# Spectral layer: where and when its tables and tokens are loaded

## The chip, the cores and the metric

The kernel runs on one core of a Trainium2 chip. The metric is device microseconds of one launch. The time before is 2777.88 us, the median of three runs (2777.81, 2777.88 and 2810.39).

## The reference

Two layers act on `x` of shape (2, 128, 64, 64). Layer 0 is a group norm with four-head attention over 4096 tokens. Layer 1 turns each image into 4096 tokens of 128 channels, adds an attention of the normed tokens with themselves, and then adds a spectral layer:

```python
t = _to_tokens(x)
t = t + _L1_attn_ref(_ln_t(t))
t = t + _L1_ffn_ref(_ln_t(t), sigma, phi, M_u, M_phi_plus, M_phi_minus, log_weights, gumbel)
```

The spectral layer convolves the tokens causally with 16 filters of length 4096, once as they are and once with alternating signs, and mixes the 16 results by 128x128 matrices; a short three-tap part is added. Four branches (all, half, a quarter, an eighth of the tokens) are combined with weights of which one is nearly 1:

```python
U_plus = jnp.fft.irfft(Vf[None, :, :, None] * Uf_p[:, :, None, :], n=n, axis=1)[:, :sl]
out = jnp.einsum('btkd,k,kde->bte', U_plus, s, Mpp)
out = out + jnp.einsum('btkd,k,kde->bte', U_minus, s, Mpm)
```

## The kernel before

The program goes in order through layer 0 for both batches, the second attention of batch 0, that of batch 1 (`attend16`), and the spectral layer. A fast version of it, called with `in_halves` true, runs; a second version stands in the program for inputs whose ranges don't fit, and isn't executed here.

**Attention.** `attend16` goes over pairs (j, i) of blocks of 512 tokens, i from j on. For each pair TensorE computes scores from `bothT` (L1185: `hiT` and `loT`, two f16 parts of the normed tokens, transposed), ScalarE takes the exponential, and the result is weighed with `hi` and `lo`, the same tokens not transposed (L1213). For i > j the block is also needed transposed: SP issues two transposing DMAs `eT<-pair` (L1204), which are used two pairs later. Between these steps it calls `next(beside, None)`, which runs one piece of side work; beside batch 1's attention that is `feed(0, ...)`.

**feed(b)** prepares the spectral layer for batch b. For each of eight groups of four token tiles it normalises (`un`), transforms by two matmuls (L1328), splits the result into two f16 parts `uh` (two buffers), stores them in DRAM as `rows16[b]` by four DMAs each, makes `uT`, and computes the three taps into `oc` (one buffer, L1308 to L1315), which is stored as `base[b]` (L1316). Its DMAs are issued by GpSimd for batch 0 (`aside`) and by SP for batch 1. In pieces: one for `un`, two with `rows` stores, one for `uT`, three for the taps, seven in all for a group.

**The spectral layer** is 64 steps: 2 batches, 2 halves `ro` of the output rows, 8 chunks `ch`, 2 signs `s`. A step needs two halves of tables (a tile of [128, 16, 8, 32] f16 each, 1 MB, read from DRAM `tables16` by one DMA) and two halves of tokens ([128, 8, 128] f16, by two DMAs of 128 KB from `rows16[b]`). `convolve16` multiplies them (16 matmuls, L1541, in four turns w of four; turns 0 and 1 use the first half, 2 and 3 the second); ScalarE and VectorE turn the results into f16 parts `x`. `mix16` then runs 48 matmuls (L1557) with the matrices `mxr` and `mxl`. The mix of a step is laid between the four turns of the next step's convolution, and one piece of side work is taken from `beside` in each turn. TensorE's order is written out: `ordered` is `tc.keep_in_program_order`, which pins an instruction behind the instruction traced just before it on its engine. Instructions that aren't pinned are placed by a planner, which lets them float to where it takes their inputs to be ready.

Side work of the first 16 steps is `feed(1, ...)`, after four empty pieces. After each (batch, ro) follows `back`, which turns the 16 chunks back into tokens: five empty pieces, then for each of four parts a load `had<-base` (L1653, one buffer), four plus four transposes, and an inverse transform (L1669) that VectorE adds to `had` (L1671). After `ro` 1 the result goes out by four DMAs.

**Loads of a step.** `chunk16(n, ...)` is called at the start of step n. Tables and tokens have two sets, by n % 2. Set 0 of the tables, `tables_a`, lies in a pool `early`, opened after batch 0's attention; set 1, `tables_b`, takes the places b0 and b1 of the pool `px`, where `hi` and `lo` lay. Tables are issued by SP (L1483), tokens by GpSimd (L1478), those of step 0 by SP. None of these DMAs is pinned. Each waits until the convolution of step n − 2 has read its half.

SP and GpSimd issue in order: an issue that waits holds back what stands behind it on that engine. `px` also has a place a, which holds `bothT` during the attentions. `transform` loads `fw` (L975) on GpSimd, and `closed(j)`, called at the end of a row of the attention, lets VectorE and GpSimd (`lrsf`, a power, L108) finish the norm of batch 1's tokens.

Of the kernel before, what the change touches and what calls it, by code (L numbers as in the profile page):

```python
# [13 lines left out]
F16 = mybir.dt.float16  # L14
# [8 lines left out]
P = 128  # L23
B, C, HH, WW = 2, 128, 64, 64
# [11 lines left out]
NK = 16  # L36
# [3 lines left out]
BP = NI // 2  # L40
NF = P
NW = NF // 4
NDI = 2 * BP - 1
# [3 lines left out]
NCH = NW // WC  # L47
NS = NF // NCH // 2
# [28 lines left out]
def conv_attn_hybrid(ctx: ExitStack, tc: tile.TileContext, io):  # L77
    nc = tc.nc
# [31 lines left out]
    def pool(stack, name, bufs=1, **kw):  # L110
        return stack.enter_context(tc.tile_pool(name=name, bufs=bufs, reuse_waits="tile", **kw))
# [5 lines left out]
    def chain(*parts):  # L117
        for p in parts:
            yield from p
# [588 lines left out]
    tables16 = dram.tile([2, NF // NS, 2, 2, 2, NDI, NS, 2 * NK], F16, name="tables16")  # L708
    rows16 = [dram.tile([2, 2, DROWS, NF, C], F16, name=f"rows16_{b}") for b in range(B)]
# [48 lines left out]
    def layers(st, layer0, in_halves):  # L758
# [3 lines left out]
        tokens = [pool(st, f"tok{b}", side="right") for b in range(B)]  # L762
        tok = [tokens[b].tile([P, NI, C], F32, tag="t", name=f"tok{b}") for b in range(B)]
        px = pool(st, "px", side="right")
# [196 lines left out]
        psum, bank = banks(psum_a)  # L961
# [18 lines left out]
        if not in_halves:  # L980
            tokens_in = ffw.tile([P, 2, 2, WC // 2, C], F32, name="tokens_in")
# [77 lines left out]
        def attend(b, p, beside, closed, ready=lambda i: None):  # L1059
# [111 lines left out]
            for _ in beside:  # L1171
                pass

        def attend16(b, p, beside, closed):

            den = p.tile([P, NT, NQ], F32, tag="den", name=f"den{b}")
# [205 lines left out]
        with ExitStack() as l1:  # L1382
            p1 = pool(l1, "l1")
            if not in_halves:
                lo.append(p1.tile([P, L], F32R, name="lo"))
            with ExitStack() as part:
                p = pool(part, "l1_a")
                gate = [0]

                def second_parts(n):  # L1390
                    if n < NQ and not in_halves:
                        low = p.tile([P, 2, 512], F32, tag="low", name=f"low{n}")
                        nc.sync.dma_start(low, lows[n].rearrange("n p c -> p n c"))
                        copy = nc.vector.tensor_copy(loT[0][:, bass.ts(n, 512)], low[:, 0])
                        if n == 0:
                            tc.keep_in_program_order(copy)
                        nc.vector.tensor_copy(lo[0][:, bass.ts(n, 512)], low[:, 1])

                def ready(i):
                    second_parts(i + 1)  # L1400

                second_parts(0)
                fw = transform(p1)

                def closed(j):
                    gate[0] = j + 1

                y = [None]

                def stage(i, n):  # L1410
                    y[0] = p.tile([P, 512], F32, tag="y", name=f"y1_{i}")
                    return y[0]

                stats = LayerStats(p1, tok[1], "a1")
                own = (rest16(p),) if in_halves else (filters(p, fw), matrices(p))
                steps = chain(left, stats.steps(), *own, normalise(1, stats, stage, gate))
                (attend16(0, p1, steps, closed) if in_halves else attend(0, p1, steps, closed, ready))
            right0.close()
            if in_halves:
                early = pool(middle, "early", side="right")  # L1420
                tables_early = [early.tile([P, BP, NS, 2 * NK], F16, name=f"tables_a{n}") for n in range(2)]
                tokens_in = [
                    [early.tile([P, NS, C], F16, name=f"tokens{turn}_{n}") for n in range(2)] for turn in range(2)
                ]
            if in_halves:
                mxr, mxl = mixing
            else:
                mxr, mxl = (x[0].rearrange("p (k s c) -> p k s c", k=NK, s=2) for x in (hiT, loT))
            with ExitStack() as part:
                p = pool(part, "l1_b", 2)  # L1430
                fed = LayerStats(ffw, tok[1], "f1")

                def closed(j):
                    fed.take(range(4 * j, 4 * j + 4))
                    fed.close(range(4 * j, 4 * j + 4))
                    own = slice(2 * j, 2 * j + 2)
                    m = p.tile([P, 2, 2, C], F32, tag="m", name=f"m{j}")
                    aside.dma_start(m, mx[own].rearrange("k p s c -> p k s c"))
                    nc.vector.tensor_copy(mxr[:, own], m)
                    nc.vector.tensor_tensor(mxl[:, own], m, mxr[:, own], ALU.subtract)  # L1440

                (attend16 if in_halves else attend)(1, p1, feed(0, p, bank, fw), closed)
        psum_a.close()


# [2 lines left out]
        late_pool = pool(right1, "late", 2, side="right")  # L1448

        if in_halves:  # L1450
            tables_in = [
                tables_early,
                [px.tile([P, BP, NS, 2 * NK], F16, tag=f"b{n}", name=f"tables_b{n}") for n in range(2)],
            ]
        else:
            tables_in = [
                px.tile([P, 2, WC // 2, 2 * BP * NK], F32, tag=f"b{n}", name=f"tables_in{n}") for n in range(2)
            ]

        def ordered(instruction):  # L1460
            return tc.keep_in_program_order(instruction)

        def one_bank(name):
            return pc.tile([P, 512], F32, tag="bk", name=name)

        STREAM = {(0, 0): 0, (0, 1): 2, (1, 0): 1, (1, 1): 0}
        FIRST = (0, BP + 1, BP)

        def chunk16(n, b, ro, ch, s):

            row = FIRST[STREAM[ro, s]]
            halves = []
            for half in range(2):
                w0 = 2 * NS * ch + NS * half
                tt = tables_in[n % 2][half]
                ut = tokens_in[n % 2][half]
                for copy in range(2):
                    (nc.gpsimd if n else nc.sync).dma_start(  # L1478
                        ut[64 * copy : 64 * copy + 64],
                        rows16[b].rearrange("h c r w d -> (h c) r w d")[:, row : row + BP, w0 : w0 + NS, :],  # L1480
                    )
                own = tables16[s, w0 // NS]
                nc.sync.dma_start(  # L1483
                    tt,
                    bass.AP(
                        tensor=own.tensor,
                        offset=own.offset,
                        ap=[[NDI * NS * 2 * NK, 8], [NS * 2 * NK, BP], [1, BP * NS * 2 * NK]],
                    ),
                )  # L1490
                halves.append((tt, ut))
            return halves

        def chunk(turn, b, ro, ch, s):


            row = FIRST[STREAM[ro, s]]
            halves = []
# [194 lines left out]
        fw = transform(late_pool)  # L1693
        beside = chain([None] * WC, feed(1, late_pool, one_bank, fw, fed))
        steps = 0
        for b in range(B):
            for ro in range(2):
                oh = (late_pool if ro else tokens[0]).tile(
                    [P, L], F32, tag="oh" if ro else "t", name=f"oh{b}_{ro}", bufs=1
                )  # L1700
                for ch in range(NCH):
                    acc = pc.tile([P, 512], F32, tag="acc", name=f"m{b}_{ro}_{ch}")
                    for s in range(2):
                        u = f"{b}_{ro}_{ch}_{s}"
                        if in_halves:
                            xs = [
                                pf.tile([P, NK, 512], F16, tag=f"x{n}", name=f"x{n}_{u}", bufs=2) for n in range(2)
                            ]
                            parts = convolve16(u, chunk16(steps, b, ro, ch, s), *xs)
                        else:  # L1710
                            halves = chunk(steps % 2, b, ro, ch, s)
                            xh = pf.tile([P, NK, WC * 4 * 2 * BP], F32R, tag="xh", name=f"xh{u}", bufs=2)
                            parts = convolve(steps, u, halves, xh)
                        for _ in parts:
                            next(late, None)
                            next(beside, None)
                        late = mix16(ch, s, *xs, acc, oh) if in_halves else mix(steps, ch, s, xh, acc, oh)
                        steps += 1
                for _ in beside:
                    pass  # L1720
                if (b, ro) == (0, 0):
                    right1.close()
                    late_pool = pool(right1, "out", 2, side="right")
                beside = back(b, ro, oh, outs, late_pool)
                if in_halves and (b, ro) == (0, 1):
                    beside = chain(beside, guard(one_bank))
# [136 lines left out]
```

## Time and profile before

The profile is of one execution that took 2786.72 us; its span, from the first to the last instruction, is 2784.9 us, at a mean granted TensorE clock of 0.977.

| what | before |
|---|---|
| median of three runs | 2777.88 us |
| profiled execution | 2786.72 us, span 2784.9 |
| first convolution of step 0 starts | 1724.7 us |
| first convolution of step 1 starts | 1746.3 us |
| `m` L1557, 3072 matmuls | 622.5 + 391.4 us busy |
| `x` L1549 on VectorE, 512 | 602.3 us busy, 1219 ns each |
| `tables_a`, `tables_b`, 64 + 64 transfers of 1 MB | issued by SP |
| `tokens`, 252 transfers of 128 KB | issued by GpSimd, 12.2 us to landing |
| `rows<-uh` of batch 1, 64 of 64 KB; `base<-oc`, 8 of 256 KB; `had<-base`, 12 of 256 KB | issued by SP |
| DMA queue of SP | 231.71 MB of 311.92 MB |

How to read such a profile: the times are microseconds from the span's start. "PE" is TensorE's matmuls, "PEld" its weight loads, "DVE" VectorE, "ACT" ScalarE, "POOL" GpSimd, "SP" SyncE; "SPq" is SP's sequencer, which issues DMAs. A name such as `tables_b<-tables` is the written tile and the read one. The chain of waits is followed back from the last instruction: at each step to what released it. A wait is put down to the releaser that came last. The windows give busy time of each engine in a stretch, the granted clock as a share of full speed, and the mean busy share of the 16 DMA engines.

### The profile page before, as it was taken

What the parts mean: (1) busy time and instruction counts of PE and PEld (TensorE: products, weight loads), DVE (VectorE), ACT (ScalarE), POOL (GpSimd) and SP (SyncE); (2) the same over time, 40 slices, a digit from 0 to 9 for tenths busy, and PEclk for the clock granted to TensorE, in tenths of its full rate; (3) what the DMA queues carried; (4) which work ended last, traced back from release to release, by engine and by line L of the source; (5) the groups of instructions that cost most, each with busy time, mean ns of one, the idle gap of its engine ahead of it and who ended that gap; (6) DMA issues with size and microseconds to landing.
All of it is one profiled execution on the core that took longest, in us unless ns stands there. A gap on an engine that the chain in (4) does not pass through costs nothing.

```text
span 2784.9 us, 32561 instructions
## 1 busy us (share of the span) xinstructions
PE 2588.1 (93%) x11955; PEld 1276.1 (46%) x11955; DVE 1668.5 (60%) x2946; ACT 1841.3 (66%) x2059; POOL 432.5 (16%) x711
## 2 busy tenths in 40 slices
PE   5999999999998996999989988898789999999998
PEld 3555555555544452444434443343344445445444
DVE  5256564246267225767886567575456666666664
ACT  4999999999998894556644555454345555555553
POOL 2022121012124201100043100111111111111110
PEclk9999999999999997999999998999999999999999
DMA  4122220012014307655375654666666666655662
GB/s 144 35 65 67 65 65 20 7 50 74 22 39 94 67 5 135 115 107 105 69 144 110 126 96 91 154 174 156 149 167 165 200 192 181 179 206 179 185 188 87
DMA packets 351051, 311.92 MB, mean 112 GB/s; under 512 B 292816, under 2 KB 303200, under 8 KB 334432
## 3 DMA queue, kind: packets, MB, share of 16 engines
q1 hardware_dynamic: 295376, 231.71, 32.6%
q0 software_dynamic: 52512, 74.81, 11.2%
q10 hardware_dynamic: 2992, 3.22, 0.4%
q8 instruction: 96, 1.57, 0.2%
q14 instruction: 75, 0.61, 0.1%
HBM read 212.53 MB, written 23.33 MB: 85 GB/s over the span
## 4 chain that ended last, share of the span: by engine, by line
PE 30%; DMA 13%; DVE 7%; issue 1%; ACT 1%; POOL 0%; SPq 0%; DVEq 0%; ACTq 0%; POOLq 0%
PE m L1557 19%; PE cv L1541 6%; DMA eT<-pair 5%; DMA tables_b<-tables 3%; DVE pair L1199 3%; DMA base<-oc 2%; DVE both L1232 2%; PE ar L1312 1%; DMA had<-base 1%; DVE x L1549 1%; PE bk L1669 1%; DMA tables_a<-tables 1%; DMA rows<-uh 1%; PE od L1213 1%; PE pf L1328 0%
## 5 line engine op out<-in xcount | busy, mean ns | idle before, releaser
L465 ACT ACTIVATE e<-s 128x1536 f16<-128x1536 f32 (+1 forms) x704 | 938.4, 1427 | 52.9 <-PE s L209 48.3
L1549 DVE TENSOR_TENSOR x<-cv,x 128x1024 f16<-128x1024 f32 x512 | 602.3, 1219 | 302.9 <-ACT x L1548 302.9
L1548 ACT CAST x<-cv 128x1024 f16<-128x1024 f32 x512 | 493.7, 1017 | 404.4 <-PE cv L1541 389.5
L1557 PE MATMUL m<-x,mxr 128*128 128x512 f16 x2048 | 622.5, 381 | 0.0
L209 PE MATMUL acc<-e,v 128*97 128x512 f16 x2048 | 559.0, 380 | 16.4 <-DVE accs L413 13.7
L209 PE MATMUL s<-qs,ks 128*128 128x512 f16 x2048 | 559.7, 380 | 7.9 <-ACT e L465 4.3
L1557 PE MATMUL m<-x,mxl 128*128 128x512 f16 x1024 | 391.4, 382 | 3.3 <-DVE oh L1564 3.2
L209 PEld LDWEIGHTS <-v 128*97 128x97 bf16 x2048 | 255.4, 125 | 229.8 <-issue 28.9
L1194 ACT ACTIVATE ey<-y,nshift 128x512 f32<-128x512 f32 x288 | 196.0, 685 | 225.3 <-PE y L1185 135.9
L1557 PEld LDWEIGHTS <-mxr 128*128 128x128 f16 x2048 | 201.3, 98 | 242.8 <-issue 5.3
L209 PEld LDWEIGHTS <-ks 128*128 128x128 f16 x2048 | 201.0, 99 | 229.6 <-issue 46.8
L1478 POOL DMA_DIRECT2D tokens<-rows x252 | 152.9, 611 | 845.5 <-PE cv L1541 819.8
L1232 DVE SCALAR_TENSOR_TENSOR both<-eT 128x512 f16<-128x512 f16 x224 | 153.6, 686 | 135.2 <-DMA eT<-pair 124.5
L1213 PE MATMUL od<-pair,hi 128*128 128x512 f16 x576 | 189.6, 391 | 30.0 <-DVE oT L1225 15.1
L1185 PE MATMUL y<-bothT 128*128 128x512 f16 x864 | 206.5, 381 | 4.0 <-ACT ey L1194 3.0
L1199 DVE TENSOR_TENSOR pair<-ey,pair 128x1024 f16<-128x1024 f32 x144 | 175.4, 1218 | 16.0 <-ACT pair L1198 15.6
L413 DVE COPY accs<-acc 97x512 f32<-97x512 f32 x64 | 44.1, 689 | 227.3 <-PE acc L209 227.1
L1541 PEld LDWEIGHTS <-tokens 128*128 128x128 f16 x1024 | 100.6, 99 | 164.5 <-issue 68.1
L1213 PEld LDWEIGHTS <-hi 128*128 128x128 f16 x1024 | 102.6, 100 | 146.2 <-issue 35.1
L1198 ACT CAST pair<-ey 128x1024 f16<-128x1024 f32 x144 | 150.2, 1043 | 24.6 <-DMA eT<-pair 11.4
L1557 PEld LDWEIGHTS <-mxl 128*128 128x128 f16 x1024 | 101.0, 99 | 131.6 <-DVE oh L1564 10.0
L1213 PE MATMUL oa<-eT,hi 128*128 128x512 f16 x448 | 146.6, 389 | 14.3 <-DMA eT<-pair 14.3
(221 smaller groups left out, 2297.5 us busy)
## 6 DMA issues: line engine op xcount, KB each, us to landing
tables_a<-tables SPq DMA_DIRECT2D x64, 1024.0 KB
tables_b<-tables SPq DMA_DIRECT2D x64, 1024.0 KB
tokens<-rows POOLq DMA_DIRECT2D x252, 128.0 KB, 12.2
tab<-in_rot SPq DMA_DIRECT2D x32, 512.0 KB
ks<-term POOLq DMA_DIRECT2D x112, 64.0 KB, 2.2
qs<-term POOLq DMA_DIRECT2D x112, 64.0 KB, 2.1
accs<-back SPq DMA_DIRECT2D x32, 128.0 KB
room<-in_mpp POOLq DMA_DIRECT2D x16, 256.0 KB, 3.4
```

The source lines that it names most:

```text
L209: tc.keep_in_program_order(nc.tensor.matmul(*args, **kw))
L465: nc.scalar.activation(e[:, own, :], ps[:, own, :], AF.Exp, scale=SCORE_SCALE)
L1185: nc.tensor.matmul(ps[:, q, :], a[0][:, bass.ts(t, P)], c[0][:, bass.ts(i, 512)], start=(n == 0), stop=(n == 2),)
L1194: nc.scalar.activation(e[:, q, :], ps[:, q, :], AF.Exp, bias=nshift16, accum_out=den[:, t, i : i + 1])
L1199: nc.vector.tensor_tensor(pair[:, 1, own], e, pair[:, 0, own], ALU.subtract)
L1213: nc.tensor.matmul(acc, a[0][:, own], pair(m, t), start=(start and t == 0 and n == 0), stop=(stop and t == 3 and n == 2),)
L1232: nc.vector.scalar_tensor_tensor(both, eT[:, 0, :, u, :], 1.0, eT[:, 1, :, u, :], ALU.mult, ALU.add, accum_out=den[:, 4 * i + u, j : j + 1],)
L1478: (nc.gpsimd if n else nc.sync).dma_start(ut[64 * copy : 64 * copy + 64], rows16[b].rearrange("h c r w d -> (h c) r w d")[:, row : row + B ...
L1541: ordered(nc.tensor.matmul(pu[:, h, :], ut[:, at, :], tt[:, :, at, :], start=True, stop=True))
L1548: nc.scalar.copy(hi, pur)
L1549: nc.vector.tensor_tensor(lo, pur, hi, ALU.subtract)
L1557: nc.tensor.matmul(acc, m, x, start=(s == 0 and i == 0), stop=(s == 1 and i == len(products) - 1))
```

## The change

`chunk16` goes. A generator `fetch16(n, queue)` and a small `halves16(n)` take its place, defined before the attention:

- Tables and tokens have three sets, by n % 3. Set 0 of the tables is in `early` as before (now `tables_e`), set 1 is one tile `second` in `px`'s place a, set 2 takes places b0 and b1. The third set of tokens is in `early`.
- Step n now begins with `fetch16(n + 1, nc.sync)`, so the loads of step n + 1 stand ahead of step n's convolution and side work. For n = 63 it returns at once.
- All loads are pinned by `ordered`. Tokens are always issued by GpSimd, tables by the queue that is given.
- `fetch16(0, nc.gpsimd)`, tables and tokens of step 0, is appended to the side work of batch 1's attention, behind `feed(0, ...)`; one piece for each half.

```diff
+        def fetch16(n, queue):
+            if n == len(STEPS):
+                return
+            b, ro, ch, s = STEPS[n]
+            row = FIRST[STREAM[ro, s]]
+            for half in range(2):
+                w0 = 2 * NS * ch + NS * half
+                tt, ut = halves16(n)[half]
+                for copy in range(2):
+                    ordered(
+                        nc.gpsimd.dma_start(
+                            ut[64 * copy : 64 * copy + 64],
+                            rows16[b].rearrange("h c r w d -> (h c) r w d")[:, row : row + BP, w0 : w0 + NS, :],
+                        )
+                    )
+                own = tables16[s, w0 // NS]
+                ordered(
+                    queue.dma_start(
+                        tt,
...
+                    )
+                )
+                yield
+
+        def halves16(n):
+            return list(zip(tables_in[n % 3], tokens_in[n % 3]))
...
-                (attend16 if in_halves else attend)(1, p1, feed(0, p, bank, fw), closed)
+                if in_halves:
+                    attend16(1, p1, chain(feed(0, p, bank, fw), fetch16(0, nc.gpsimd)), closed)
+                else:
+                    attend(1, p1, feed(0, p, bank, fw), closed)
...
-            tables_in = [
-                tables_early,
-                [px.tile([P, BP, NS, 2 * NK], F16, tag=f"b{n}", name=f"tables_b{n}") for n in range(2)],
-            ]
+            second = px.tile([P, 2, BP, NS, 2 * NK], F16, tag="a", name="tables_a")
+            tables_in.append([second[:, n] for n in range(2)])
+            tables_in.append([px.tile([P, BP, NS, 2 * NK], F16, tag=f"b{n}", name=f"tables_b{n}") for n in range(2)])
...
-        def chunk16(n, b, ro, ch, s):
...
-                for copy in range(2):
-                    (nc.gpsimd if n else nc.sync).dma_start(
...
-                            parts = convolve16(u, chunk16(steps, b, ro, ch, s), *xs)
+                            for _ in fetch16(steps + 1, nc.sync):
+                                pass
+                            parts = convolve16(u, halves16(steps), *xs)
```

## The prediction

> **What bounds the kernel now.** I read the page first: what is busy, and at which clock.
>
> ```profile
> span 2784.9 us, 32561 instructions
> PE 2588.1 (93%) x11955; PEld 1276.1 (46%) x11955; DVE 1668.5 (60%) x2946; ACT 1841.3 (66%) x2059; POOL 432.5 (16%) x711
> PE   5999999999998996999989988898789999999998
> PEclk9999999999999997999999998999999999999999
> ```
>
> TensorE is busy 93%; the weak slices inside are the 16th (1044 to 1114 us) and most from the 24th to the 30th (1601 to 2089). In the 16th layer 0 ends and batch 0's second attention starts; the spectral layer runs from 1724.6 to the end. The windows say how much TensorE time lies idle where (columns: stretch, length, busy of each engine, granted clock, DMA share, GB/s).
>
> ```profile
> 1098.40:1109.00 10.60, 1.03 (x3) 0.25 (x2) 0.00 (x0) 0.88 (x4) 0.00 (x0) 0.66 0.74 147
> 1724.60:1746.20 21.60, 7.20 (x19) 1.97 (x17) 13.06 (x31) 7.90 (x8) 4.55 (x6) 0.62 0.59 131
> 1752.00:2124.80 372.80, 336.33 (x1508) 159.12 (x1506) 226.29 (x241) 169.14 (x192) 48.45 (x80) 0.97 0.62 160
> 2124.80:2291.70 166.90, 166.28 (x769) 74.86 (x768) 114.82 (x100) 93.93 (x99) 29.08 (x48) 1.00 0.61 192
> 2371.90:2420.10 48.20, 43.83 (x194) 18.94 (x193) 28.91 (x26) 23.12 (x24) 7.27 (x12) 0.96 0.60 173
> 2420.10:2743.40 323.30, 322.27 (x1537) 152.12 (x1536) 222.30 (x195) 178.32 (x190) 50.91 (x84) 1.00 0.58 182
> ```
>
> Fourth and sixth row: where steps have little side work, idle is under 0.4%, and nothing can be won. What can be won is idle 9.6 us (first row), 14.4 (second), 36.5 (third), 4.4 (fifth), 65 in all, and some slow clock. TensorE's waits from 1720 on and the chain name the releasers.
>
> ```profile
> PE cv L1541 <- DMA tables_b<-tables: 24.8, 8, 12.3
> PE ar L1312 <- ACT oc L1308: 11.5, 3, 8.2
> PE cv L1541 <- DMA tables_a<-tables: 7.5, 3, 2.9
> ...
> 1723.93 22.22 DMA tables_b<-tables
> ...
> 1889.39 23.22 DMA base<-oc
> ...
> 2029.06 29.16 DMA tables_b<-tables
> ```
>
> Tables cost 32.3 us directly. `oc` waits for its own store, which took 23.2 us for 256 KB because SP's queue also held tables. Last, SP's issues in order of time, early and at the border:
>
> ```profile
> 1084.26 1.48 SPq L1483 DMA_DIRECT2D tables_a<-tables  x2
> 1087.73 51.21 SPq L1204 DMA_TRANSPOSE eT<-pair  x9
> ...
> 1708.12 4.74 SPq L1204 DMA_TRANSPOSE eT<-pair  x2
> 1723.28 1.24 SPq L1483 DMA_DIRECT2D tables_b<-tables  x2
> 1729.87 4.68 SPq L1483 DMA_DIRECT2D tables_a<-tables  x2
> ```
>
> Step 0's tables are issued at 1084, 640 us before use and just ahead of transposes that batch 0's attention needs at once; step 1's only at 1723.3.
>
> The packet records of the trace add a rate: a half of a step's tables is 128 packets of 8,192 bytes, and the halves pass SP's queue one after another. From the first packet of step 1 (1724.7) to the last of step 21's first-issued half pair (2121.0) 42 halves pass; the queue is empty between halves for 13.4 us in all. So a half takes (396.3 − 13.4) / 42 = 9.1 us, two 18.2, while a step with side work takes TensorE 16.4 to 17.3 where it doesn't stall. In that stretch the tables' stream itself is about as long as TensorE's work. Later, alone, a half takes 5.5 to 8.5 us and a bare step 13.8.
>
> **The change part by part.** The sum is made against the profiled execution: 2786.72 us (span 2784.9), 8.8 above the median 2777.88; I take the difference over to the median unchanged.
>
> *Step 0's tables leave 1084.* Gone: 9.6 us idle at 1098.4 to 1109, 1.1 in the 7 us behind it, and about 3 of half clock (6.9 us busy at 0.54 to 0.66). Without the 2 MB, the stretch 1160 to 1200 still idles 2.3 in 40, 0.6 per 10. Gain 11; bounds 5 (the stall is partly the transposes' own) and 13.
>
> *They come back on GpSimd beside batch 1's attention,* at about 1572 to 1580, when the first feed ends: four token issues (0.61 us each, as in L1478's row) and two of tables on POOL, which is busy 1.3 us of the 10 from 1570 on. Behind them in POOL's order wait the next `lrsf` power (next due 1617) and `fw`, with 40 us to spare. SP loses four token issues (2.24 us at 1547). The 2 MB are wanted at 1724: landing costs nothing. What they do to the transposes isn't in the trace. From below: 0, being in another queue than the transposes. From above: 14, all that the same bytes cost at 1084. I take 4, nearer the lower end, since at 1084 the halves took 20.9 us and the transposes stood behind all of it in one queue. The Trainium skill's "DMA: Bandwidth & Descriptors" (Queues, rings and completion order) speaks against this part: all queues share the same engines, which take turns between queues by packets. By that rule the transposes would go at half rate for some 20 us, an estimate of 10 instead of 4, and the sum would be 6 smaller.
>
> *Step 1 moves to the buffer of `bothT`* (tag a), whose last reader is the last L1185 at 1710.3 to 1713.0; before, it waited for `hi` and `lo`, read until 1723.4. SP has nothing between its last transposes (1708.1) and this. So the issue moves from 1723.3 to 1713. Step 1's tokens hang behind `fw`'s load on POOL (1577 before), so they remain early. Step 1 began at 1746.3, right behind its second half (last packet 1744.6); I expect 1736, when x of step 0 is done (DVE until 1736.6). Counted in the next part.
>
> *Three sets, issued ahead of side work.* What it doesn't remove is bytes. A fetch of step n+1 is pinned behind the SP transfers traced in step n−1 and no longer waits for step n−1's matmuls, only for step n−2's. The stream begins at 1714.4 instead of 1724.7 and loses its empty stretches. With 42 halves at 9.1 it would end at 2097, at 9.9 at 2130. 9.9 is the mean of the 14 halves issued within 0.9 us of each other (8.1 to 12.3), and pairs are what the new order issues beside side work. I take 9.4: 1714.4 + 395 = 2109; step 21 needs the first of its halves, 9.4 earlier, plus 1.6 to signal it: 2101 against 2124.8. Gain 23 for this part and step 1 together. Bounds: 3 (at 9.9: 2122) and 66 (no stall: 14.4 + 36.5 idle, 15 slow clock at 0.62, 0.65 and 0.97). The page's section Bandwidth gives 6.15 us for 1 MB; by that 42 halves would take 258 us, an estimate, and the sum would be that of the first rival. The rows here (0.52 to 0.62 of the engines' time, 125 to 160 GB/s) decide against it.
>
> *Side transfers then queue behind tables.* What is behind a fetch on SP: the `rows`, `base` and `had` transfers of its own step; what is ahead: those of the step before. A `base` store stands behind one fetch's rest, as now, so its present cost (11.5 us) stays inside the sum; more of it is the slow rival.
>
> *Step 38 to 40:* idle 4.4, where `out` stores fill the queue; one more step of lead (some 14 us, against waits of 2 to 3) covers it. Gain 4 (0 to 5). Bare steps: the halves are still freed 6.9 us apart; no change. Register and instruction counts of TensorE, DVE and ScalarE stay.
>
> Sum: 11 + 23 + 4 − 4 = 34; 2786.7 − 34 = 2753 for a profiled execution, 2744 for the median.
>
> **The rivals.** *TensorE alone bounds the layer.* The third set lets halves overlap side work so freely that they run at the later rate (5.5 to 8.5 us each). For it: halves 12 to 15 took 5.9 to 8.7 in the middle of side work. Against: most there took 8.1 or more. Then 56 of the 66 go (10 stay for `oc` and `uh`): 11 + 56 + 4 − 3 = 68, median 2710.
>
> *The stream stays the bound.* Pairs at 9.9: gain 3; GpSimd's 2 MB cost 10: 11 + 3 + 4 − 10 = 8, median 2770. This is also the case that the change doesn't do what it says: the tables are asked for sooner, and arrive no sooner.
>
> *Slower: stores and loads of side work stuck behind two whole fetches.* `oc` has one buffer; from its store to the next write are five of the seven turns of a row group, 5 × 4.3 = 21.5 us. The three stores in the chain took 22.3 to 23.2 and cost 11.5; from 21.5 on, every microsecond of queue is TensorE's. `had` has one buffer too: twice it took 14.3 to 16.6, and VectorE waited up to 6.1. If all 7 later stores cost 8.2 and the 9 later loads of the three turns 6.1, that is 57 + 55 − 24 (paid now: 11.5 and 12.8) = 88 more. Against 11, 4 and 10 (step 1), and 4 lost: 67 slower, median 2845.
>
> **How the numbers follow.** Chances: forecast 0.46 (its own range 2725 to 2765), TensorE alone 0.22 (2700 to 2725), stream 0.18, slower 0.14 (2785 to 2860). The range 2704 to 2785 holds the forecast, the stream rival and nearly all of the fast rival, and leaves out the slow one. 2% is 55.6 us, about what a measurement of this kernel can tell from no change: faster than 2722 is the fast rival but its edge, and the forecast's tail, 0.24; slower than 2833 is somewhat over half of the slow rival, 0.08; the rest 0.68.
>
> **What would show it.** Step 0's tables on POOL near 1575, and no idle of 9 us near 1100: part one. A wait for `eT` over 5 us soon after 1575: its cost. Step 1 beginning 10 us after step 0's last convolution or less: the border. From there to step 21, the interval, 378.5 now from step 1, near 365 with the queue never empty: the stream; near 325: the fast rival; waits on `oc` or `had` above 30 us in sum: the slow one. I am wrong if the halves' mean leaves 8.5 to 9.9 us, or if the scheduler moves attention's own work when it places the new transfers.

## The result, and the profile after

The changed kernel takes 2805.89 us (median of 20 executions, 2782.06 to 2828.83); the kernel before, beside it, 2788.08 (20 executions, 2771.6 to 2814.15). The ratio is 1.0059, with a 95% interval of 1.0033 to 1.0084: slower by under 1%, where 2744 us was predicted and 2785 was the upper end of the range. Ratios here leave out, on both sides, executions more than 1.5% above the fastest of their kernel, so they are not exactly the quotient of the medians.

The profiled execution of the changed kernel took 2782.06 us, the lowest of its 20, so its total flatters it. A second profile of the same code, called "again" below, took 2804.88 (span 2803.1) and is near the median. The page of the first:

```profile
span 2780.2 us, 32560 instructions
...
PE 2586.0 (93%) x11955; PEld 1275.8 (46%) x11955; DVE 1669.1 (60%) x2946; ACT 1841.9 (66%) x2059; POOL 437.3 (16%) x717
...
PE   5999999999999997989989689899999999999998
...
PEclk9999999999999998999999899999999999999999
```

In the row of TensorE (PE) the weak slice where layer 0 ends is better (the 16th, 7 instead of 6), and a new hole stands in the 23rd slice (the 6, at 1529 to 1599 us), inside batch 1's attention. The windows of the changed kernel, cut where the work changes, tell more. The columns are the stretch, its length, busy time of TensorE, of weight loads, of VectorE, ScalarE and GpSimd, then clock, DMA share and GB/s.

```profile
1043.20:1354.20 311.00, 276.87 (x1269) 126.13 (x1268) 234.09 (x537) 174.27 (x360) 17.57 (x20) 0.96 0.56 107
1556.70:1739.70 183.00, 145.61 (x649) 64.40 (x648) 107.65 (x249) 87.41 (x180) 13.97 (x21) 0.93 0.70 110
1739.70:1749.50 9.80, 6.54 (x19) 1.86 (x18) 9.74 (x25) 7.08 (x8) 3.31 (x4) 0.72 0.52 116
1749.50:2110.40 360.90, 337.47 (x1525) 160.94 (x1525) 232.73 (x249) 172.10 (x195) 49.84 (x82) 0.98 0.62 166
```

And the same windows of "again", where step 1 to step 21 is the last row:

```profile
1047.70:1357.90 310.20, 277.94 (x1268) 126.18 (x1268) 233.77 (x537) 174.36 (x360) 17.55 (x20) 0.96 0.57 107
1559.90:1742.50 182.60, 147.29 (x649) 64.86 (x648) 107.67 (x249) 87.23 (x180) 13.94 (x21) 0.92 0.70 110
...
1752.30:2138.00 385.70, 346.98 (x1525) 163.04 (x1525) 232.13 (x249) 171.58 (x195) 49.43 (x82) 0.95 0.62 156
```

Beside the kernel before, in us:

| stretch | before | changed | again |
|---|---|---|---|
| batch 0's second attention | 323.1 | 311.0 | 310.2 |
| 217th score block of batch 1 to step 0 | 155.2 | 183.0 | 182.6 |
| step 0 to step 1 | 21.6 | 9.8 | 9.8 |
| step 1 to step 21 | 378.5 | 360.9 | 385.7 |
| step 21 to step 40 | 280.9 | 290.7 | 283.6 |
| step 40 to step 63 | 330.4 | 331.0 | 333.3 |

So the gain of 12 in batch 0 and of 12 at the border is there. Batch 1's attention gives 27 to 28 back, and from step 1 on nothing is won for certain: the two profiles of one program differ by 25 us in steps 1 to 21. In "again", the one near the median, the rows add up to a loss of 15.5 us.

The waits of TensorE in the changed kernel, from 1740 us on:

```profile
PE cv L1554 <- DMA tokens<-rows: 12.0, 6, 4.4
PE cv L1554 <- DMA tables_e<-tables: 8.0, 5, 3.2
PE cv L1554 <- DMA tables_a<-tables: 6.8, 3, 3.1
PE cv L1554 <- DMA tables_b<-tables: 5.5, 3, 2.7
```

Together 32.3 us; before, tables alone were 24.8 + 7.5 = 32.3. The wait for `oc`, 11.5 before, is gone. And in batch 1's attention TensorE waits for transposes. From 1280 to 1740 us in the changed kernel:

```profile
PE oa L1254 <- DMA eT<-pair: 23.4, 4, 17.0
```

and from 1280 to 1724 us in the kernel before:

```profile
PE oa L1213 <- DMA eT<-pair: 0.9, 1, 0.9
```

The cause stands in the order of time. GpSimd's issues in the changed kernel (start, duration):

```profile
1558.13 1.31 POOL L1194 DMA_DIRECT2D tokens<-rows  x2
1559.43 0.60 POOL L1201 DMA_DIRECT2D tables_e<-tables  x1
1561.10 1.23 POOL L1194 DMA_DIRECT2D tokens<-rows  x2 [1.07 <-issue]
1562.32 0.60 POOL L1201 DMA_DIRECT2D tables_e<-tables  x1
...
1577.56 1.82 POOL L1194 DMA_DIRECT2D tokens<-rows  x3 [7.38 <-DMA tables_e<-tables]
```

and the chain that ended last, in the same kernel, with the transposes that it passes through:

```profile
1547.53 5.03 DMA eT<-pair
...
1558.38 12.28 DMA eT<-pair
...
1584.26 19.54 DMA eT<-pair
...
1642.70 4.31 DMA eT<-pair
```

A transpose that takes 4.3 us later in the same attention takes 12.3 and 19.5 while GpSimd's tables and tokens pass; the next block pairs wait. Besides the 2 MB of tables and step 0's tokens, GpSimd issues eight loads there, the tokens of steps 1 and 2 (the x3 in the row at 1577.56 are some of them). Those of step 1 were loaded in the kernel before too, at 1563.5, ahead of this stretch, which begins at 1569.5 there; those of step 2 come this early because there is a third set.

### The profile page after: what moved, and what is told of

Same layout as the page of the kernel before. It is cut to its first block, busy times and chain, and to the rows that moved or that the text cites. A ratio compares the mean times of both kernels' runs of the same rounds, so it can differ in the third digit from the quotient of the medians.

```text
span 2780.2 us, 32560 instructions
## 1 busy us (share of the span) xinstructions
PE 2586.0 (93%) x11955; PEld 1275.8 (46%) x11955; DVE 1669.1 (60%) x2946; ACT 1841.9 (66%) x2059; POOL 437.3 (16%) x717
## 4 chain that ended last, share of the span: by engine, by line
PE 55%; DMA 20%; DVE 14%; ACT 7%; issue 3%; SPq 0%; POOL 0%; DVEq 0%; ACTq 0%; POOLq 0%
PE m L1570 18%; PE acc L209 11%; PE s L209 11%; DMA eT<-pair 9%; PE cv L1554 6%; ACT e L465 5%; DVE pair L1240 4%; DMA tables_e<-tables 3%; DVE both L1273 3%; DMA tables_b<-tables 2%; PE od L1254 1%; DMA tables_a<-tables 1%; PE y L1226 1%; PE ar L1353 1%; DMA tokens<-rows 1%
## 5 line engine op out<-in xcount | busy, mean ns | idle before, releaser
L1240 DVE TENSOR_TENSOR pair<-ey,pair 128x1024 f16<-128x1024 f32 x144 | 175.5, 1219 | 16.6 <-ACT pair L1239 16.3
```

The costliest lines, as they stand in the source:

```text
L1240: nc.vector.tensor_tensor(pair[:, 1, own], e, pair[:, 0, own], ALU.subtract)
```

## The experiments

The interval in each is of its ratio to the kernel before, run beside it. A stretch is read from one profile of each, and "again" shows how far two profiles of one program lie apart: 0.4 us in the stretch before step 0, 25 us from step 1 to 21. The edits are shown in part; `...` stands for what is left out. `free` in them returns an instruction unpinned.

**1. The changed kernel once more.** No edit.

> The changed kernel once more, for a second look at where its time lies. Theory A: the 2 MB that GpSimd loads beside batch 1's attention delay the transposes that this attention waits for, in every execution. Then the stretch from the 217th score block of batch 1 to step 0 again takes 175 to 195 us (155.2 before, 183.0 in the profile after), with waits for eT of 15 to 30 us, and the median lies 5 to 25 us above that of the kernel before. Rival B: that stall is an accident of the profiled execution; then the stretch takes 155 to 165 us.

Median 2805.55, ratio 1.0049 (1.0007 to 1.0091). The waits for `eT` (25.9 us in sum, the longest 16.7), the 182.6 us and the border (9.8) repeat, so these parts are not chance. Steps 1 to 21 don't repeat (385.7 against 360.9).

**2. Step 0's loads by SP, early, as before; three sets and early issue kept.**

```diff
-                    attend16(1, p1, chain(feed(0, p, bank, fw), fetch16(0, nc.gpsimd)), closed)
+                    attend16(1, p1, feed(0, p, bank, fw), closed)
...
+        if in_halves:
+            for _ in fetch16(0, nc.sync, nc.sync, free):
+                pass
```

> The changed kernel with one part undone: step 0's tables and tokens are issued by SP and not pinned, as in the kernel before; the three sets and the pinned order of all other steps stay. Theory A: the stall beside batch 1's attention goes (28 us less there) and that at 1098 us comes back (12 us more): 16 us less than the changed kernel, 5 to 10 us less than the kernel before. Rival B (GpSimd's load is innocent; the planner placed the attention's work worse): same as the changed kernel within 5 us.

Ratio 1.0046 (1.0012 to 1.0081): the total did not fall. The stretch before step 0 fell from 183.0 to 164.1, and batch 0's stall came back (324.4 against 311.0). What is won in one place is lost in the other: step 0's loads cost 13 beside one attention and 19 beside the next. 9 us above the 155.2 of before stay, with GpSimd issuing the eight loads of tokens of steps 1 and 2 at 1572 to 1578, inside the stretch.

**3. Only step 0's loads on GpSimd; two sets and the old order for the rest.**

```diff
...
-            return list(zip(tables_in[n % 3], tokens_in[n % 3]))
+            return list(zip(tables_in[n % 2], tokens_in[n % 2]))
...
-                            for _ in fetch16(steps + 1, nc.sync):
+                            for _ in fetch16(steps, nc.sync, pin=free) if steps else ():
```

> The kernel before with one part done: only step 0's tables and tokens move to GpSimd behind the first feed; two sets, and all other loads unpinned and issued in their own step, as before. Theory A: 12 us gained in batch 0's attention, 28 lost in batch 1's, 16 us slower than the kernel before. Rival B: no stall over 5 us in batch 1's attention, 8 to 12 us faster than the kernel before.

Ratio 1.0063 (1.003 to 1.0096). Batch 0's attention 312.0, stretch before step 0 172.4: 11 won, 17 lost. Of later tokens only step 1's are loaded about here, at 1550, ahead of the stretch, as in the kernel before. So step 0's tables, with their four loads of tokens, cost 17, and with the 9 of run 2 that makes 26 of the 27.8. The rest of the loss lies from step 1 on, where steps 1 to 21 took 385.9 us.

**4. The fetches not pinned from step 1 on.**

```diff
-                            for _ in fetch16(steps + 1, nc.sync):
+                            for _ in fetch16(steps + 1, nc.sync, pin=free):
```

> The changed kernel with the pins taken from the loads of steps 1 to 63, so that the planner may put them ahead of the side work's transfers; three sets as in the change. Theory C: beside side work the third set does nothing because each fetch stands on SP behind the stores of the step before (issued 22 to 42 us after its set was free, in steps 3 to 16). Then the unpinned loads are issued within 10 us of that, TensorE's waits for tables and tokens fall from 32 us to under 12, and steps 1 to 21 take 345 us or less instead of 361. Rival D: the rate of the tables' stream is the bound; then steps 1 to 21 stay within 6 us of 361.

Ratio 1.0101 (1.0045 to 1.0156), no better than the change. Its profiled execution, 2832.99 us, was the slowest of its six (median 2815.8), so its stretches are on the long side; the one before step 0 took 194.8, with 36.7 us of waits for `eT`, though the edit leaves step 0's loads alone, and why is not shown. Tables are now issued soon after their set is free (0 to 29 us later, mostly under 14, against 22 to 42 in steps 3 to 14 of the changed kernel) and land 15 to 34 us ahead of use. TensorE's waits for tables fall to 7.5 us from 1700 on, and steps 1 to 21 take 394 us all the same. Its longest waits from 1740 to 2160 us:

```profile
PE ar L1356 <- ACT oc L1352: 17.7, 5, 6.7
PE vt L1675 <- DVE out L1687: 13.9, 1, 13.9
PE pf L1372 <- DVE uh L1345: 13.1, 1, 13.1
```

`oc`, `had` (which is added into `out`) and `uh` each wait until their own transfer has landed, behind tables in SP's queue: ScalarE waited 39.2 us for `base<-oc` and 22.7 for `rows<-uh`, VectorE 17.5 for `had<-base`. This is the mechanism of the prediction's slow rival: whichever of the two goes first, the other is late. That points at the queue itself as too slow; the next runs test it.

**Why is it too slow?** The trace's packet records say how many of a half's packets of 8,192 bytes are under way at a time. While any is, the commonest count is 8 in the kernel before and in the changed one, though the profile's page counts 16 DMA engines. The tables' DMA has 8 entries in its outermost dimension. The next runs ask for that, and for the lump on GpSimd.

**5. Step 0's tables in 16 pieces of 128 KB by SP, one per block pair.**

```diff
+                for piece in range(pieces):
+                    rows_ = slice(P // pieces * piece, P // pieces * (piece + 1))
...
+                                ap=first + [[NS * 2 * NK, BP], [1, BP * NS * 2 * NK]],
...
+                    for _ in range(4 if n == 0 else 1):
+                        yield
...
-                    attend16(1, p1, chain(feed(0, p, bank, fw), fetch16(0, nc.gpsimd)), closed)
+                    attend16(1, p1, chain(feed(0, p, bank, fw), fetch16(0, nc.sync)), closed)
```

> The changed kernel with the tables of step 0 issued by SP instead of GpSimd, in 16 DMAs of 128 KB (16 partitions each), one for each block pair of batch 1's attention, each pinned behind the transposes of its pair. Question: is the 28 us that the stretch from the 217th score block of batch 1 to step 0 grew (155.2 to 183.0) the price of the bytes, or of their coming in one lump of 2 MB (with step 1's and step 2's tokens, 1 MB more, issued by GpSimd right behind)? Theory A (a lump: SP's transposes wait while it passes, and TensorE waits for eT): spread out, the tables cost little and only the tokens' share stays, so the stretch is 160 to 168, as in the run where step 0's tables came early by SP (164.1), and the waits for eT there are under 8 us; median 10 to 20 below the changed kernel. Theory B (any byte beside the transposes costs its time): 2 MB at some 110 GB/s are about 18 us of queue, and the stretch stays at 178 to 188.

Median 2791.34, ratio 0.9993 (0.9956 to 1.003). The stretch is 164.0: Theory A. TensorE's waits for `eT` from 1260 to 1740 us:

```profile
PE oa L1259 <- DMA eT<-pair: 4.9, 4, 2.3
```

The same bytes cost nothing here, and the 9 of the tokens stay. But the edit changes three things at once: the bytes are spread out, they go by SP's queue, and a piece has 16 entries outermost (`BP`; `first` is empty for step 0) where a half had 8. Which of them did it, this run doesn't tell.

**6. Sixteen entries outermost.** The same bytes; a half is two DMAs of [16][4][4096] elements instead of one of [8][16][4096], and tokens are cut alike.

```diff
...
-                            ap=[[NDI * NS * 2 * NK, 8], [NS * 2 * NK, BP], [1, BP * NS * 2 * NK]],
...
+                                ap=[[NS * 2 * NK, BP], [NDI * NS * 2 * NK, 4], [1, BP * NS * 2 * NK]],
...
```

> The changed kernel with the same bytes of tables and tokens cut in another way: partitions in the order (copy, row, h c), so that the outermost of a DMA's dimensions has 16 entries instead of 8; a half of the tables is two DMAs of 512 KB. In the traces so far never more than 8 of a half's 128 packets were under way at a time (sum of packet times over the half's duration 4.7 to 7.9), though there are 16 DMA engines. Theory A (a half is held to 8 engines, and that is what makes a half 8 to 12 us beside side work): up to 16 packets at a time, a half in 5 to 7 us; waits for tables and tokens from 1750 on fall from 32 us to under 12; steps 1 to 21 in 335 to 350 us instead of 361 (profile) or 386 (again). Theory B (the rate is that of memory or of all traffic together, 125 to 160 GB/s): more packets at a time, each longer in proportion; halves stay at 8 to 11 us; steps 1 to 21 within 10 us of 361 to 386. The stretch before step 0 stays 170 to 190 by both, or longer by A, since the lump then sits on all engines.

Median 2723.72, ratio 0.9759 (0.9721 to 0.9798). From 1740 us on TensorE waits for no table and no token. Its windows, with the stretch before step 0 and steps 1 to 21:

```profile
1554.20:1727.20 173.00, 144.19 (x649) 64.09 (x648) 107.53 (x249) 87.40 (x180) 13.42 (x23) 0.95 0.69 122
1737.00:2067.90 330.90, 329.88 (x1525) 159.96 (x1525) 232.75 (x249) 171.48 (x195) 41.14 (x82) 1.00 0.76 183
```

In the second row 1.0 us is idle in 330.9. Theory A. In the first row the lump on GpSimd still costs: 173.0 against 155.2, so sixteen entries alone don't take its price away. SP still waits for ScalarE, VectorE and the stores before it issues a fetch, as in the changed kernel; in its waits from 1728 to 2110, `base` stores stand 89.6 us for `oc` and `rows` stores 74.0 for `uh`. With a half in 5.2 us (1.05 MB at the 200 GB/s of the table under run 11) instead of 9, that lateness no longer costs TensorE a wait.

**7. The queues parted:** from step 1 on tables and tokens by SP, side work's transfers by GpSimd.

```diff
-            queue = aside if b == 0 else nc.sync
+            queue = aside
...
-                        nc.gpsimd.dma_start(
+                        (queue if n else nc.gpsimd).dma_start(
...
-                    nc.sync.dma_start(had, baser[:, ro, 4 * p4 : 4 * p4 + 4, :])
+                    aside.dma_start(had, baser[:, ro, 4 * p4 : 4 * p4 + 4, :])
```

> The changed kernel with the queues parted: from step 1 on SP issues nothing but tables and tokens; the stores rows and base of batch 1's feed and the loads had go to GpSimd. Step 0's tables stay on GpSimd as in the change. Theory A (loads come late because they are pinned on SP behind the stores of the step before, which wait for ScalarE and VectorE; without the pin, stores and had loads queue behind 2 MB): with both gone, a fetch is issued within 5 us of its set coming free, a step's halves land 12 us or more ahead of use, and waits for tables, tokens, oc and had together from 1750 to 2125 fall below 15 us (changed kernel about 30 over 1710 to 2780): steps 1 to 21 in 335 to 350 us. Theory B (the tables' rate itself is the bound, 9 to 10 us a half): issue is early, but steps 1 to 21 stay at 360 or more, and the halves follow each other without a gap. Also: the tokens of steps 1 and 2 now stand behind the transposes on SP, so by the decomposition tables 17 + tokens 9 the stretch from the 217th score block to step 0 falls from 183 to about 172.

Median 3127.45, ratio 1.1187 (1.113 to 1.1245). Both theories had the issue early, and it was not: SP issued mostly 30 to 37 us after the set came free. It waited little for other engines; its own issues took long (two loads of tokens 9.32 us at 1865.11, where two on GpSimd take 1.22), as they would with a full queue. Halves follow each other without a gap, so Theory B holds in that, but I had expected some 360 us, not these:

```profile
1745.30:2174.00 428.70, 354.86 (x1525) 163.35 (x1525) 233.28 (x249) 173.30 (x196) 56.03 (x79) 0.94 0.51 141
2591.40:3087.20 495.80, 376.63 (x1568) 163.08 (x1569) 227.15 (x198) 182.89 (x194) 2.25 (x3) 0.90 0.47 124
```

The second row is 23 steps with little side work: 21.6 us a step, where the kernel before takes 14.4. Tokens ahead of tables in one queue add to the time of a half (a half every 10.8 us), at half of the engines' time. The stretch before step 0 is 175.5, near the 172 expected without the tokens of steps 1 and 2.

**8. Runs 5 and 7 together.**

> Both of the edits before together: step 0's tables in 16 pieces by SP, queues parted. If the two are independent: stretch before step 0 at 155 to 162 (before 155.2), batch 0's stall gone as in the change, steps 1 to 21 as in the run with parted queues. If that run's Theory A holds, the median is 25 to 50 us below the kernel before; if its Theory B holds, 5 to 20 us below it.

Ratio 1.1112 (1.1058 to 1.1166): the misfortune of run 7 stays. But the stretch before step 0 is 155.2, that of before, with 0.5 us of waits for `eT`: with the tables in pieces by SP and the tokens of steps 1 and 2 away, nothing is left of the 27.8.

**9. The kernel before, with nothing but the new cut.**

> The kernel before, with nothing of the change, but its tables and tokens cut as in the run with sixteen rows outermost (median 2723.72, against 2805 for the change and 2788 to 2794 for the kernel before). Theory A (the cut alone does it; three sets and the early issue bring almost nothing): waits for tables and tokens from step 1 on below 6 us in sum, steps 1 to 21 in 330 to 340 us (that run 330.9), no lump beside batch 1's attention (155 us instead of 173), batch 0's stall still there but at most 12, step 0 to step 1 16 to 22 us: 2724 - 18 + (5 to 12) + (6 to 12), so 2715 to 2730. Theory B (a fast stream still needs the third set): table waits of 15 us or more from step 1 on, median 2735 to 2750.

Median 2700.7, ratio 0.9687 (0.9661 to 0.9712): better than expected, and better than run 6. Windows: batch 0's attention, the stretch before step 0, step 0 to 1, and steps 1 to 21.

```profile
1046.80:1357.70 310.90, 277.44 (x1269) 126.17 (x1268) 234.23 (x537) 174.11 (x360) 17.54 (x20) 0.96 0.60 113
1555.50:1708.30 152.80, 141.31 (x650) 63.91 (x649) 107.92 (x250) 87.24 (x180) 5.33 (x7) 0.99 0.54 101
1708.30:1718.00 9.70, 5.54 (x18) 1.64 (x16) 9.64 (x24) 7.04 (x8) 3.09 (x4) 0.84 1.01 215
1718.00:2050.10 332.10, 331.05 (x1524) 160.21 (x1524) 232.75 (x249) 171.62 (x195) 41.48 (x82) 0.99 0.82 187
```

Two sets, late issue, step 0's tables at the start of batch 0's attention: all as before, and yet every stall that the change was about is gone, batch 0's and the border's too.

**10. The change with the new cut, its lump in pieces, and the tokens of steps 1 and 2 by SP.**

> The change with sixteen rows outermost, and with what hurt beside batch 1's attention taken away: step 0's tables by SP in 16 pieces of 128 KB, one per block pair, and the tokens of steps 1 and 2 issued by SP behind the last transposes instead of by GpSimd at 1560. Expected if the cost there is the lump of tables (17 to 20) plus those tokens (9): the stretch from the 217th score block to step 0 is 154 to 160 us (sixteen alone 173.1), all else as in that run: median 2703 to 2712. If the tokens on SP delay step 1, the interval from step 0 to step 1 rises above 12.

Median 2701.92, ratio 0.9693 (0.9668 to 0.9719), stretch before step 0 151.5. The change with its own costs taken out, and it is no better than run 9.

**11. Two DMAs for a half, but four entries outermost.**

```diff
...
+                                ap=[[NDI * NS * 2 * NK, 4], [NS * 2 * NK, BP], [1, BP * NS * 2 * NK]],
...
```

> The change with each half of the tables as two DMAs of 512 KB, as in the run with sixteen rows outermost, but with four entries outermost instead of sixteen; tokens as in the change. It tells what made that run fast: the smaller DMAs, or the count of the outermost dimension. Theory A (the outermost count sets how many packets go at a time): 4, at most 8 packets under way if two DMAs overlap; a half takes 10 us or more, waits for tables at 32 us or above, median 2800 or more, over 2900 if the two DMAs do not overlap. Theory B (two DMAs in flight, or smaller ones, do it): median within 15 of 2724.

Median 3294.4, ratio 1.1813 (1.1783 to 1.1843): Theory A, with next to no overlap of the two DMAs. Steps 1 to 21, and the waits for tables from 1700 to 2800 us (the span ends at 3302.5):

```profile
1752.10:2279.70 527.60, 379.55 (x1525) 169.98 (x1525) 232.18 (x249) 172.01 (x195) 49.48 (x82) 0.84 0.36 114
```

```profile
PE cv L1555 <- DMA tables_e<-tables: 91.6, 19, 11.8
PE cv L1555 <- DMA tables_b<-tables: 79.7, 20, 9.1
PE cv L1555 <- DMA tables_a<-tables: 76.6, 20, 11.0
```

From the packet records of four kernels, for packets of 8,192 bytes between step 1 and step 21:

| kernel | outermost | commonest count under way | mean ns of a packet | share of time with any | GB/s in that time |
|---|---|---|---|---|---|
| before | 8 | 8 | 479 | 0.95 | 118 |
| changed / again | 8 | 8 / 8 | 452 / 491 | 0.93 / 0.93 | 123 / 117 |
| run 6 | 16 | 16 | 552 | 0.64 | 200 |
| run 11 | 4 | 4 | 365 | 0.96 | 82 |

The count follows the outermost dimension, and not the number or the size of the DMAs. A packet takes longer when more are under way, but far less than in proportion. Run 6 also changed the order in which rows are read; run 11 keeps the old order and has small DMAs too, and is slow. No run changes the order alone, but the gain did not come from shorter packets (552 ns against 479): more go at a time.

## Why the prediction was wrong

A gain of 34 us was forecast and 18 were lost (medians 2805.89 and 2788.08), 52 apart. In "again", the profile near the median, 23 of these are the price of step 0's tables on GpSimd, 18 the gain of three sets, and 10 steps 21 to 63.

*Step 0's tables leave 1084: right.* 12 us won, 11 predicted. Run 9 says that they need not have left: with sixteen entries outermost they cost nothing there.

*They come back on GpSimd: this term failed, 4 instead of 27 to 28, beyond the upper bound of 14.* It is the one miss that both profiles show alike. Step 0's tables and tokens are 17 to 20 of it (runs 3 and 7 against before), the tokens of steps 1 and 2 are 9 (runs 2 and 5). The bound failed twice. It took the price at 1084 as the worst, as if another queue could only be kinder; and it left out step 2's four loads of tokens, which the third set lets GpSimd issue there, and that step 1's four now follow step 0's lump, inside the stretch. The page's rule that queues share the engines by packets had the direction right, with its estimate of 10 for the tables alone. That the bytes need not cost anything is shown by runs 5, 8 and 10. Whether it is the lump or GpSimd's queue that makes them cost is not shown: in these runs the pieces went by SP, with 16 entries outermost. With that cut a lump by SP cost nothing at 1084 (run 9), and one by GpSimd, with its tokens, still cost 18 beside batch 1's attention (run 6), but these are two places.

*Step 1 at place a: right in its gain, by another clock time.* The border fell from 21.6 to 9.8, but because batch 1's attention ended later, step 1 began at 1749.5 and not at 1736.

*Three sets, issued ahead: here the mechanism failed.* It said that a continuous stream at 9.4 us a half would win 23 us with the border. From step 0 to step 21 the kernel before takes 400.1 us, the changed one 370.7 in the first profile and 395.5 in "again": a gain of 29 in the one and of 5 in the other, so two profiles don't settle the number. The rate was no worse than assumed (the prediction's 42 halves took 8.6 us each in the first profile and 9.0 in "again"). But the stream did not become continuous in either: from the first to the last of these halves, 24.0 and 28.6 us pass with no table packet under way, and 19.6 in the kernel before (every gap counted, inside a half too). SP's own waits between 1728 and 2110 show why, in the changed kernel:

```profile
SPq L1375 <- ACT uh L1341: 65.4, 9, 19.1
SPq L1357 <- DVE oc L1356: 57.4, 8, 15.1
SPq L1201 <- PE cv L1554: 41.5, 11, 9.2
SPq L1666 <- DMA had<-base: 33.5, 4, 12.6
```

and in the kernel before:

```profile
SPq L1483 <- PE cv L1541: 94.7, 21, 16.3
...
SPq L1334 <- ACT uh L1300: 26.4, 6, 6.6
...
SPq L1316 <- DVE oc L1315: 12.5, 5, 4.4
```

Before, SP waited above all for a set to come free. Now it waits at the stores of the step before for ScalarE and VectorE, and the pinned fetch stands behind them: in steps 3 to 14 of the first profile it is issued 22 to 42 us after its set was free, and its last packet lands only 0.7 to 7 us ahead of use. I had named that order ("pinned behind the SP transfers traced in step n−1") and not asked what those transfers wait for. So beside the side work the third set is hardly used. Undoing the pin (run 4) moves the waits to `oc`, `uh` and `had`.

*Steps 38 to 40: not won.* The 4 us forecast here did not come: steps 21 to 40 took 9.8 and 2.7 us longer than before, and in the first profile TensorE waited 8.4 us for tokens between 2110 and 2400.

*The rivals.* "The stream stays the bound", at 0.18, comes nearest: with the lump at 28 its sum is 11 + 3 + 4 − 28 = −10, a loss of 10; the medians lost 18. "TensorE alone bounds" would have come with a faster stream, as run 6 shows. The slow one needed the pin away.

*What was not seen.* The sum took 9 us for a half as a given. A DMA share of 0.62 in a stretch that waits for DMA was in the first windows, and it could have been asked which engines were idle. The Trainium skill's "DMA: Bandwidth & Descriptors" (section "Why a DMA increments its semaphore by 16 and not by 1") states that the number of engines of one DMA is the largest up to 16 that divides the outermost sizes of both sides, which for these tables gives 8. The counts of 4, 8 and 16 above agree. The prediction weighed the page's Bandwidth section instead.

What stays open: whether step 0's tables cost so much beside batch 1's attention because they came in a lump or because they came by GpSimd; and the 25 us between two profiles of the changed kernel from step 1 to 21. Packets took 452 ns in one and 491 in the other, and no run here tells why.

## What to carry to other kernels

A stretch that waits for transfers while the DMA engines show 0.6 busy may be short of neither buffers nor lead, as here. Count how many packets of one transfer are under way at a time, and cut the transfer so that its outermost dimension lets all engines in, before changing any order. A load moved to a quiet place is not free because it has time; here a lump of 2 MB on GpSimd held back the small transfers that the attention lives on, and sixteen pieces by SP, one per block pair, did not. An issue that is pinned is as late as the slowest wait of what it is pinned behind.

## What the runs showed of the hardware

- In these kernels, packets of 8 KB under way follow the outermost dimension of the DMA: 4, 8 and 16, with 82, 118 and 200 GB/s.
- Two DMAs of 512 KB in one queue, four entries outermost each, hardly overlapped: at most 6 packets were under way, mostly 4 (run 11).
- A transpose of 4.3 us took 12.3 and 19.5 while 2 MB of tables, and tokens, passed in another queue.
- Tokens and tables in one queue with these cuts cost 10.8 us for a half and its tokens; in two queues a step without side work took 14.4 us (330.4 for 23 steps, kernel before).
